# Routing stage of a linear-attention and mixture-of-experts layer: reordered input loads, layer-norm statistics by half blocks, one 1/sqrt per block, weight loads interleaved with the token stores

## The chip, the core and the metric

One core of one Trainium2 chip runs the whole program. The metric is the device time of one execution in microseconds (us). The kernel before was run three times: 717.43, 720.52 and 724.11 us, median 720.52 us.

The core has a matrix engine (TensorE, PE in the profile; its weight loads are shown as PEld), a vector engine (VectorE, DVE), an activation engine (ScalarE, ACT), a general engine (GpSimd, POOL) and SyncE (SP), which here only issues DMAs. Each engine executes its own instructions strictly in the order in which the program emitted them. DMAs issued by SyncE go on one hardware queue (q1 in the profile), those issued by ScalarE on another (q10).

## The reference

The input x has 4 x 1024 tokens of 256 channels. What matters here:

```python
xn = layernorm(x)                       # over 256 channels
# attention branch on xn: q, k, v projections, causal linear attention in
# chunks, a memory branch with gates, output projection w_o
# expert branch on xn:
logits = xn @ gate_weight.T             # 8 experts
scores = softmax(logits); topk_w, topk_idx = top_k(scores, 2)
topk_w = topk_w / (sum(topk_w) + 1e-20)
y  = sum over the two experts of topk_w * swiglu(xn, w_gate, w_up, w_down)
y += swiglu(xn, sw_gate, sw_up, sw_down)          # shared expert, all tokens
out = x + attention(xn) + y
```

The layer norm is (x - mean) / sqrt(var + 1e-5) for each token.

## The kernel before, in words

All arithmetic is fp32. The 4096 tokens are cut into 8 blocks (NBLK) of 512 (TB), each of 4 tiles (NT) of 128 tokens. The order of instructions on every engine is the order of the program text; no planner moves them. The kernel has four stretches:

1. **Loads** (lines 104 to 144). SyncE issues the eight blocks of x (512 KB each, L104), then the memories, gate, biases and most weights (L115 to L144). ScalarE issues `wvg` (value and expert-gate weights), `wq` and `wk`. On SyncE every store that follows comes behind all of these.
2. **The routing stage**, written out by hand as a list of steps, `ahead` (L1197). `S` is `statistics` of a block: four times bn_stats (L303) and bn_aggr (L304) on VectorE, an addition of epsilon (L309), and the power -1/2 on GpSimd (L312). Before the change, the addition and the power are done for two blocks at a time (blocks 1+2, 3+4, 5+6; 0 and 7 alone). `N` is `normalize`: a small `shift` (L319), two tiles normalized in place on VectorE (L326) and two on ScalarE (L331), and then one DMA that stores the block's normalized tokens to the DRAM tensor `xns` (L335), from which the experts later gather their rows. `T` is `transpose_x`: eight TensorE transposes by way of PSUM (L344), copied by ScalarE to `xnT` (L347). `V` is `values`: for each pair of tiles eight matmuls with `wvg` (L362), whose result ScalarE copies (L367, L371); GpSimd fills in ones and zeros (L372, L373). `masks`, `memories`, `gates`, `living` and `route` are small computations put between. The result of `pv` has two PSUM buffers (`ps_v`), each for one pair of tiles.
3. **Queries, keys, shared expert and sorting** (L1233 to L1237), in which TensorE projects queries and keys (L600) into four rotating PSUM banks (`ps_r`), ScalarE and VectorE turn them into elu(x)+1 (L605, L606, L614, L618), and VectorE sorts tokens into expert slots (`route(1)`, `sort`, `weights`, `owners`). In front of it SyncE issues the copies of x into the DRAM tensor `sums` and two fills from the SBUF tile `zero`:

```python
    for blk in range(NBLK):
        rows = slice(blk * TB, (blk + 1) * TB)
        nc.sync.dma_start(sums[rows, :], x[rows, :])
    nc.sync.dma_start(sums[T:, :], zero[:, :H])
    nc.sync.dma_start(xns[T:, :], zero[:, :H])
```

4. **Attention rounds with the routed experts beside them** (L1240 on), the bulk of the time.

Two sharings of buffers matter. The values of a block are written over its normalized tokens: `va` is a view of the tile `wide` that holds `xb`, so L367, L372 and L373 of a block have to wait until its `xns` store has read the block. And `zero` is one of three rotating buffers with the tag `wide` in the pool `tmp`, which the temporaries `eq` and `ek` of L605 use afterwards, so one of these has to wait until the last DMA that reads `zero` has finished.

Of the kernel before, what the change touches and what calls it, by code (L numbers as in the profile page):

```python
# [22 lines left out]
def linear_attention_moe_kernel(  # L23
# [28 lines left out]
    nc = tc.nc  # L52
    T, H = x.shape
    S = T // B
    NH = memory_gate.shape[1]
# [7 lines left out]
    FR = E * F  # L63
    FT = w_gate.shape[1]
    FS = FT - FR
# [3 lines left out]
    HID = eg_w1.shape[1]  # L69
    NBLK = T // TB  # L70
# [5 lines left out]
    NMN = 1 + NM  # L76
# [4 lines left out]
    const = ctx.enter_context(tc.tile_pool(name="const", bufs=1))  # L81
# [3 lines left out]
    small = ctx.enter_context(tc.tile_pool(name="small", bufs=2))  # L85
# [14 lines left out]
    def load_x(blk):  # L100

        wide = big.tile([P, NT, VW], FP, tag="tok", name=f"x_{blk}")
        xb = wide[:, :, :H]
        nc.sync.dma_start(  # L104
            xb, x[blk * TB : (blk + 1) * TB, :].rearrange("(n p) h -> p n h", p=P)
        )
        st["x", blk] = xb
        st["wide", blk] = wide

    for blk in range(NBLK):  # L110
        load_x(blk)

    def load_weight(w, name, engine=nc.sync):
        t = const.tile([P, NC, w.shape[1]], FP, tag=name, name=name)
        engine.dma_start(t, w.rearrange("(k p) c -> p k c", p=P))  # L115
        return t

    wvg = load_weight(w_vg, "wvg", nc.scalar)
    wq = load_weight(w_q, "wq", nc.scalar)
    wk = load_weight(w_k, "wk", nc.scalar)  # L120
    raw = const.tile([P, NC, NMN, D1], FP, tag="raw", name="raw")
    nc.sync.dma_start(
        raw[:, :, 1:NMN, :], memories.rearrange("(c p) m k -> p c m k", p=P)
    )
    gate = const.tile([P, NH], FP, tag="gate", name="gate")
    nc.sync.dma_start(gate, memory_gate.to_broadcast([P, NH]))
    b2 = const.tile([P, 1], FP, tag="b2", name="b2")
    nc.sync.dma_start(b2, eg_b2.to_broadcast([P, 1]))
    w1 = load_weight(eg_w1, "w1")
    b1 = const.tile([P, HID], FP, tag="b1", name="b1")  # L130
    nc.sync.dma_start(b1, eg_b1.rearrange("h o -> o h").to_broadcast([P, HID]))
    w2 = const.tile([P, HID], FP, tag="w2", name="w2")
    nc.sync.dma_start(w2, eg_w2.rearrange("h o -> o h").to_broadcast([P, HID]))
    wo = load_weight(w_o, "wo")
    wg = load_weight(w_gate[:, FR:], "wg")
    wu = load_weight(w_up[:, FR:], "wu")
    wd = const.tile([P, NF, H], FP, tag="wd", name="wd")
    full = FS // P
    nc.sync.dma_start(
        wd[:, :full, :],  # L140
        w_down[FR : FR + full * P, :].rearrange("(f p) h -> p f h", p=P),
    )
    if full < NF:
        nc.sync.dma_start(wd[: FS - full * P, full, :], w_down[FR + full * P :, :])  # L144


    zero = tmp.tile([P, TB], FP, tag="wide", name="zero", bufs=3)
# [6 lines left out]
    make_identity(nc, ident)  # L154
    ones = const.tile([P, P], FP, tag="ones", name="ones")
    nc.gpsimd.memset(ones, 1.0)
    neghalf = const.tile([P, 2 * NT], FP, tag="neghalf", name="neghalf")
    nc.gpsimd.memset(neghalf, -0.5)

    first = const.tile([P, E], FP, tag="first", name="first")  # L160
# [66 lines left out]
    ungate = const.tile([P, NH], FP, tag="ungate", name="ungate")  # L227
    gates = const.tile([P, H], FP, tag="gates", name="gates")

    def sigmoid(v):  # L230

        nc.scalar.activation(v, v, AF.Exp, scale=-1.0)
        nc.vector.tensor_scalar(v, v, 1.0, None, ALU.add)
        nc.vector.reciprocal(v, v)

    def masks():

        for r in range(2):
# [3 lines left out]
        for c in range(NC):  # L242
            nc.vector.tensor_copy(own_s[:, c], own[:, :, None].to_broadcast([P, HC, D1]))

    def gates_of_heads():
        nc.vector.tensor_scalar(gate, gate, -80.0, None, ALU.max)
        sigmoid(gate)
        nc.vector.tensor_scalar(ungate, gate, -1.0, 1.0, ALU.mult, ALU.add)
        nc.vector.tensor_copy(
            gates.rearrange("p (h k) -> p h k", k=HD), gate[:, :, None].to_broadcast([P, NH, HD])  # L250
        )
        nc.vector.tensor_scalar(b2, b2, 0.5, None, ALU.mult)
# [37 lines left out]
        nc.vector.tensor_scalar(alive, tot[:, :NMN], EPS, None, ALU.is_ge)  # L290


    def statistics(blk):

        xb = st["x", blk]
        if blk == 0 or blk % 2:
            st["mv"] = small.tile([P, 2, NT, 2], FP, tag="mv", name=f"mv_{blk}", bufs=3)
            st["rstd"] = small.tile([P, 2, NT], FP, tag="rstd", name=f"rstd_{blk}", bufs=3)
        mv, rstd = st["mv"], st["rstd"]
        at = (blk + 1) % 2 if blk else 0  # L300
        for i in range(NT):
            stats = small.tile([P, 6], FP, tag="stats", name=f"stats_{blk}_{i}")
            nc.vector.bn_stats(stats, xb[:, i, :])  # L303
            nc.vector.bn_aggr(mv[:, at, i, :], stats)  # L304
        st["norm", blk] = mv[:, at], rstd[:, at]
        if blk % 2 == 0 or blk == NBLK - 1:
            n = at + 1
            some = rstd[:, :n].rearrange("p b i -> p (b i)")
            nc.vector.tensor_scalar(  # L309
                some, mv[:, :n, :, 1].rearrange("p b i -> p (b i)"), LN_EPS, None, ALU.add  # L310
            )
            nc.gpsimd.tensor_tensor(some, some, neghalf[:, : n * NT], ALU.pow)  # L312

    def normalize(blk):

        xb = st["x", blk]
        mv, rstd = st.pop(("norm", blk))
        shift = small.tile([P, NT], FP, tag="shift", name=f"shift_{blk}")
        nc.vector.scalar_tensor_tensor(  # L319
            shift, mv[:, :, 0], -1.0, rstd, ALU.mult, ALU.mult  # L320
        )
        xnT = io.tile([P, NC, TB], FP, tag="xnT", name=f"xnT_{blk}")
        st["xnT", blk] = xnT
        half = NT // 2
        for i in range(half, NT):
            nc.vector.tensor_scalar(  # L326
                xb[:, i, :], xb[:, i, :], mv[:, i, 0:1], rstd[:, i : i + 1],
                ALU.subtract, ALU.mult,
            )
        for i in range(half):  # L330
            nc.scalar.activation(  # L331
                xb[:, i, :], xb[:, i, :], AF.Identity,
                bias=shift[:, i : i + 1], scale=rstd[:, i : i + 1],
            )
        nc.sync.dma_start(  # L335
            xns[blk * TB : (blk + 1) * TB, :].rearrange("(n p) h -> p n h", p=P), xb
        )

    def transpose_x(blk, pair):
        xb, xnT = st["x", blk], st["xnT", blk]  # L340
# [34 lines left out]
    def route(half):  # L375

        n = NTT // 2
        part = slice(half * n, (half + 1) * n)
        lg = lgs[:, part, :]
        sh = [P, n, E]  # L380

        def t2(name):
            return small.tile([P, n], FP, tag=name, name=f"{name}_{half}", bufs=2)

        def spread(t):
            return t[:, :, None].to_broadcast(sh)
# [12 lines left out]
        nc.vector.tensor_reduce(best, lg, AX.X, ALU.max)  # L399
        m1, m2 = (pick[r][:, part, :] for r in range(2))  # L400
        yield from first_largest(lg, best, m1, "m1")
        rest = small.tile(sh, FP, tag="rest", name=f"rest_{half}", bufs=1)
        nc.vector.scalar_tensor_tensor(rest, m1, -1e30, lg, ALU.mult, ALU.add)
        low = t2("low")
        nc.vector.tensor_reduce(low, rest, AX.X, ALU.max)
        yield from first_largest(rest, low, m2, "m2")
        st["best", half] = best
# [773 lines left out]
    def split(units, parts):  # L1181
# [12 lines left out]
        return runs  # L1194


    ahead = "S0 S1 masks N0 T0 S2 S3 N1 N2 V0 T1 T2 S4 memories V1 S5 N3 N4 V2 T3 T4 S6 gates V3 S7"  # L1197
    ahead += " N5 N6 V4 living T5 T6 N7 V5 route V6 T7 V7"
    other = {
        "masks": masks, "memories": memories_by_group, "gates": gates_of_heads, "living": living,  # L1200
        "route": lambda: [None for _ in route(0)],
    }
    with tc.tile_pool(name="ps_v", bufs=2, space=bass.MemoryType.PSUM) as ps_v:
        for what in ahead.split():
            if what in other:
                other[what]()
                continue
            blk = int(what[1:])
            if what[0] == "S":
                statistics(blk)  # L1210
            elif what[0] == "N":
                normalize(blk)
            else:
                for pair in range(NT // 2):
                    (transpose_x if what[0] == "T" else values)(blk, pair)

    ps_q = ctx.enter_context(tc.tile_pool(name="ps_q", bufs=1, space=bass.MemoryType.PSUM))
    quad = ps_q.tile([P, NG, 512], FP, tag="quad", name="quad")
# [128 lines left out]
```

## Time and profile before

| | |
|---|---|
| median of three runs | 720.52 us (717.43 to 724.11) |
| the profiled execution | 720.73 us, of which the span from first to last instruction is 718.8 us |
| mean granted TensorE clock | 0.97 |
| PE busy | 656.1 us, 91% of the span |
| PEld, DVE, ACT, POOL busy | 468.4, 455.8, 266.9, 385.6 us |
| DMA bytes over the span | 81.50 MB |
| first transposes start (L344) | 11.24 us |
| last value matmuls end (L362) | about 59.2 us |

The profile is one execution. The timeline lists instructions by start time (us from the span's start), then duration, engine, source line, operation and tiles (written<-read), and in brackets how long the engine had been idle and what ended the idle time. Neighbouring equal instructions are merged ("x8"), so a merged row's duration runs from the first start to the last end. "SPq" and "ACTq" are instructions that issue DMAs. Rows by window give each engine's busy time in a stretch, then the granted TensorE clock as a share of full speed and the DMA throughput.

### The profile page before, as it was taken

How to read it: one execution, taken by the hardware profiler on the slowest of the kernel's cores; microseconds unless marked ns; L12 is line 12 of the kernel's file. 1: busy time of each engine (PE TensorE's matmuls, PEld its weight loads, DVE VectorE, ACT ScalarE, POOL GpSimd, SP SyncE). 2: the span in 40 equal slices, each digit the busy share in tenths (PEclk: the TensorE clock that was granted, in tenths of full speed). 3: DMA queues.
4: the chain of work that ended last, by engine and by line, in shares of the span. 5: the costliest groups of instructions: out<-in, count | busy, mean ns of one | idle time of the engine just before them, and what ended most of it. 6: DMA issues, size and time to landing. Idle time of an engine off the chain costs nothing.

```text
span 718.8 us, 14242 instructions
## 1 busy us (share of the span) xinstructions
PE 656.1 (91%) x5084; PEld 468.4 (65%) x5084; DVE 455.8 (63%) x1193; ACT 266.9 (37%) x614; POOL 385.6 (54%) x436
## 2 busy tenths in 40 slices
PE   3699987888999999999999999999999987998987
PEld 2585465675676667766676766676767765665666
DVE  6544888886675656665756665657656654454764
ACT  3365443333433343334333442344333433243310
POOL 3210034455465566565664564646665777666576
PEclk9899988999999999999999999999999999699999
DMA  9556000014344444443444453535445676575285
GB/s 295 175 189 190 1 1 1 1 29 115 86 108 102 111 98 89 103 119 86 115 108 91 108 107 77 123 91 116 111 96 123 136 182 145 123 157 126 30 269 206
DMA packets 86466, 81.50 MB, mean 113 GB/s; under 512 B 7533, under 2 KB 83997, under 8 KB 86269
## 3 DMA queue, kind: packets, MB, share of 16 engines
q1 hardware_dynamic: 70797, 60.14, 29.1%
q0 software_dynamic: 13632, 18.62, 15.2%
q10 hardware_dynamic: 1968, 1.84, 0.7%
q8 instruction: 40, 0.66, 0.4%
q14 instruction: 29, 0.24, 0.1%
HBM read 62.62 MB, written 22.15 MB: 118 GB/s over the span
## 4 chain that ended last, share of the span: by engine, by line
PE 71%; DMA 9%; DVE 8%; POOL 4%; ACT 4%; issue 3%; SPq 0%; ACTq 0%; POOLq 0%; DVEq 0%
PE phe L1052 11%; PE pye L1065 7%; PE psu L921 6%; PE po L958 6%; PE pg L907 5%; DMA sums<-y,islot 4%; PE quad L691 4%; PE pn L717 4%; PE po L962 4%; PE quad L806 3%; PE pk L600 3%; PE pq L600 3%; PE pv L362 2%; PE pte L1039 2%; PE pte L1043 2%
## 5 line engine op out<-in xcount | busy, mean ns | idle before, releaser
L1074 POOL DMA_INDIRECT sums<-y,islot x71 | 113.3, 1595 | 80.0 <-DMA sums<-y,islot 28.4
L1052 PE MATMUL phe<-wgu,turned 128*128 128x352 f32 x276 | 99.5, 484 | 2.5 <-ACT turned L1045 1.2
L1058 DVE SCALAR_TENSOR_TENSOR hidden<-hidden,phe 128x176 f32<-128x176 f32 x71 | 23.8, 335 | 117.8 <-ACT hidden L1057 113.2
L698 DVE TENSOR_TENSOR sT<-quad,causal 128x512 f32<-128x512 f32 x128 | 80.6, 681 | 8.1 <-PE quad L691 7.8
L1006 POOL DMA_INDIRECT xg<-xns,islot x71 | 70.3, 990 | 19.7 <-issue 10.6
L1065 PE MATMUL pye<-wdn,turned 88*128 88x256 f32 x284 | 77.3, 395 | 1.8 <-issue 1.4
L828 POOL TENSOR_TENSOR cg<-coarse,gates 128x256 f32<-128x256 f32 x32 | 24.5, 767 | 98.0 <-DVE h L885 53.5
L1052 PEld LDWEIGHTS phe<-wgu,turned 128*128 128x128 f32 x276 | 49.5, 195 | 27.0 <-issue 8.3
L1065 PEld LDWEIGHTS pye<-wdn,turned 88*128 88x128 f32 x284 | 51.2, 194 | 15.3 <-issue 6.7
L1069 ACT ACTIVATE y<-pye,wslot 128x256 f32<-128x256 f32 x71 | 33.6, 473 | 70.8 <-PE pye L1065 59.0
L1045 ACT COPY turned<-pte 128x512 f32<-128x512 f32 (+1 forms) x71 | 41.0, 578 | 46.7 <-PE pte L1043 43.1
L846 POOL TENSOR_TENSOR fm<-fm 128x512 f32<-128x512 f32 x32 | 44.0, 1374 | 26.7 <-DVE prob L894 16.6
L1057 ACT ACTIVATE hidden<-phe 128x176 f32<-128x176 f32 x71 | 22.5, 317 | 71.3 <-PE phe L1052 67.6
L958 PE MATMUL po<-wd,h 128*128 128x256 f32 (+1 forms) x192 | 47.4, 383 | 0.1
L907 PE MATMUL pg<-xnT,wg 128*128 128x512 f32 (+1 forms) x96 | 47.4, 617 | 0.0
L921 PE MATMUL psu<-xnT,wu 128*128 128x512 f32 (+1 forms) x96 | 47.0, 613 | 0.2 <-DVE skT L618 0.2
L835 DVE TENSOR_TENSOR fm<-quad,rw 128x512 f32<-128x512 f32 x64 | 41.9, 680 | 0.0
L560 POOL TENSOR_TENSOR held<-ones,two 128x213 f32<-128x213 f32 (+1 forms) x22 | 16.0, 736 | 44.9 <-DVE ones L540 44.9
L896 DVE SCALAR_TENSOR_TENSOR o<-diff,prob,loc 128x256 f32<-128x256 f32 x32 | 37.4, 1167 | 3.4
L362 PE MATMUL pv<-wvg,xnT 128*128 128x264 f32 x128 | 32.9, 418 | 7.0 <-ACT xnT L347 7.0
L958 PEld LDWEIGHTS po<-wd,h 128*128 128x128 f32 (+1 forms) x192 | 34.9, 190 | 6.4 <-issue 0.4
L806 PE MATMUL quad<-mem,sqT 32*128 32x170 f32 x512 | 28.9, 341 | 7.6 <-DVE sT L698 7.5
(210 smaller groups left out, 1376.1 us busy)
## 6 DMA issues: line engine op xcount, KB each, us to landing
wgu<-in_w_gate_dram SPq DMA_DIRECT2D x71, 176.0 KB
wgu<-in_w_up_dram SPq DMA_DIRECT2D x71, 176.0 KB
wdn<-in_w_down_dram SPq DMA_DIRECT2D x71, 176.0 KB
x<-in_x_dram SPq DMA_DIRECT2D x8, 512.0 KB
xns<-x SPq DMA_DIRECT2D x8, 512.0 KB
sums<-in_x_dram SPq DMA_DIRECT2D x8, 512.0 KB
part<-sums SPq DMA_DIRECT2D x12, 256.0 KB
out_dram<-acc SPq DMA_DIRECT2D x12, 256.0 KB
```

The source lines that it names most:

```text
L362: nc.tensor.matmul(pv[:, j, : H + E], xnT[:, k, i * P : (i + 1) * P], wvg[:, k, :], start=(k == 0), stop=(k == NC - 1),)
L600: nc.tensor.matmul(pq, w[:, k, c * P : (c + 1) * P], xnT[:, k, :], start=(k == 0), stop=(k == NC - 1),)
L698: nc.vector.tensor_mul(sT, quad[:, g, :].rearrange("p (c t) -> p c t", t=P), causal[:, None, :].to_broadcast([P, NC * 2, P]),)
L806: nc.tensor.matmul(quad[:, g, c * KM : (c + 1) * KM], sqT[rows, c, tok], mem[rows, c, :], start=True, stop=True,)
L846: nc.gpsimd.tensor_add(fm[:, :, 0:2, :], fm[:, :, 0:2, :], fm[:, :, 2:4, :])
L907: nc.tensor.matmul(pg[:n, :], wg[:, k, f * P : f * P + n], xnT[:, k, :], start=(k == 0), stop=(k == NC - 1),)
L921: nc.tensor.matmul(pu[:n, :], wu[:, k, f * P : f * P + n], xnT[:, k, :], start=(k == 0), stop=(k == NC - 1),)
L958: nc.tensor.matmul(po[:, :H], st["h", blk, f][:k, tok], wd[:k, f, :], start=(f == 0), stop=False)
L1006: nc.gpsimd.indirect_dma_start(out=xg, out_offset=None, in_=xns, in_offset=bass.IndirectOffsetOnAxis(ap=islot[:, j : j + 1], axis=0),)
L1052: nc.tensor.matmul(ph[:, : 2 * F], xgT[:, k, :], wgu[:, k].rearrange("p g f -> p (g f)"), start=(k == 0), stop=(k == NC - 1),)
L1065: nc.tensor.matmul(py[:, :H], hT[:FH, f, :], wdn[:, f, :], start=(f == 0), stop=(f == 1))
L1074: nc.gpsimd.indirect_dma_start(out=sums, out_offset=bass.IndirectOffsetOnAxis(ap=islot[:, j : j + 1], axis=0), in_=st.pop(("y", j)), in_of ...
```

## The change

- Block 0 of x is loaded as two halves, the first on SyncE's queue, the second on ScalarE's. `wvg` follows on ScalarE's queue.
- All other constants are no longer issued behind x. They are collected in a list, `loads`, in a new order, and `normalize` issues two of them after every `xns` store. So on SyncE the stores come right behind the x loads.
- `statistics` works on half a block (two tiles) at a time; epsilon and the power are done once for every block, after its second half.
- The list `ahead` is new: the halves stand about the normalizations, values go pair by pair with the next block's transposes between them, and `masks`, `memories`, `living`, `route` and `gates` are put elsewhere.
- The exponential of the head gates becomes a step of its own (`exps`), apart from what VectorE does with it (`gates`).

```diff
+        parts = 2 if blk == 0 else 1
+        n = NT // parts
+        for part in range(parts):
+            rows = slice((blk * NT + part * n) * P, (blk * NT + (part + 1) * n) * P)
+            (nc.scalar if part else nc.sync).dma_start(
+                xb[:, part * n : (part + 1) * n],
+                x[rows, :].rearrange("(n p) h -> p n h", p=P),
+            )
...
+    def load_weight(w, name, engine=None):
+        t = const.tile([P, NC, w.shape[1]], FP, tag=name, name=name)
+        src = w.rearrange("(k p) c -> p k c", p=P)
+        if engine is None:
+            loads.append(lambda: nc.sync.dma_start(t, src))
+        else:
+            engine.dma_start(t, src)
+        return t
+
+    load_x(0)
+    wvg = load_weight(w_vg, "wvg", nc.scalar)
+    for blk in range(1, NBLK):
         load_x(blk)
...
-    def statistics(blk):
+    def statistics(blk, half):
...
+        n = NT // 2
+        for i in range(half * n, (half + 1) * n):
             stats = small.tile([P, 6], FP, tag="stats", name=f"stats_{blk}_{i}")
             nc.vector.bn_stats(stats, xb[:, i, :])
-            nc.vector.bn_aggr(mv[:, at, i, :], stats)
...
+            nc.vector.bn_aggr(mv[:, i, :], stats)
+        if half:
+            nc.vector.tensor_scalar(rstd, mv[:, :, 1], LN_EPS, None, ALU.add)
+            nc.gpsimd.tensor_tensor(rstd, rstd, neghalf, ALU.pow)
...
         nc.sync.dma_start(
             xns[blk * TB : (blk + 1) * TB, :].rearrange("(n p) h -> p n h", p=P), xb
         )
+        for _ in range(2):
+            if loads:
+                loads.pop(0)()
...
-    ahead = "S0 S1 masks N0 T0 S2 S3 N1 N2 V0 T1 T2 S4 memories V1 S5 N3 N4 V2 T3 T4 S6 gates V3 S7"
-    ahead += " N5 N6 V4 living T5 T6 N7 V5 route V6 T7 V7"
+    ahead = "S0a S0b S1a N0 T0 S1b S2a N1 V0a T1 V0b S2b S3a N2 V1a T2 V1b masks S3b S4a N3 V2a T3 V2b"
+    ahead += " memories S4b S5a N4 V3a T4 V3b living S5b S6a N5 V4a T5 V4b route exps S6b S7a N6 V5a T6"
+    ahead += " V5b S7b N7 V6a T7 V6b gates V7a V7b"
```

The order of `loads` is: memories (`raw`), gate; wq, wk; b2, wg; wu, w1; b1, w2; wo, the first part of wd; the rest of wd. So the store of block 0 has the first two behind it, that of block 1 the next two, and so on; block 7's has none.

More of the change, by code (lines that the diff above doesn't have):

```diff
@@ L103, in load_x @@
         xb = wide[:, :, :H]
-        nc.sync.dma_start(
-            xb, x[blk * TB : (blk + 1) * TB, :].rearrange("(n p) h -> p n h", p=P)
-        )
+        parts = 2 if blk == 0 else 1
[6 more added lines that the diff above has]
+            )
@@ L107, in load_x @@
         st["x", blk] = xb
         st["wide", blk] = wide
-    for blk in range(NBLK):
-        load_x(blk)
[L113 to L120, printed above, removed]
+    loads = []
+    def load_weight(w, name, engine=None):
[6 more added lines that the diff above has]
+        return t
@@ L121, in linear_attention_moe_kernel @@
+    load_x(0)
+    wvg = load_weight(w_vg, "wvg", nc.scalar)
+    for blk in range(1, NBLK):
+        load_x(blk)
     raw = const.tile([P, NC, NMN, D1], FP, tag="raw", name="raw")
-    nc.sync.dma_start(
-        raw[:, :, 1:NMN, :], memories.rearrange("(c p) m k -> p c m k", p=P)
+    loads.append(
+        lambda: nc.sync.dma_start(
+            raw[:, :, 1:NMN, :], memories.rearrange("(c p) m k -> p c m k", p=P)
+        )
     )
     gate = const.tile([P, NH], FP, tag="gate", name="gate")
-    nc.sync.dma_start(gate, memory_gate.to_broadcast([P, NH]))
+    loads.append(lambda: nc.sync.dma_start(gate, memory_gate.to_broadcast([P, NH])))
@@ L127, in linear_attention_moe_kernel @@
+    wq = load_weight(w_q, "wq")
+    wk = load_weight(w_k, "wk")
     b2 = const.tile([P, 1], FP, tag="b2", name="b2")
-    nc.sync.dma_start(b2, eg_b2.to_broadcast([P, 1]))
+    loads.append(lambda: nc.sync.dma_start(b2, eg_b2.to_broadcast([P, 1])))
+    wg = load_weight(w_gate[:, FR:], "wg")
+    wu = load_weight(w_up[:, FR:], "wu")
     w1 = load_weight(eg_w1, "w1")
     b1 = const.tile([P, HID], FP, tag="b1", name="b1")
-    nc.sync.dma_start(b1, eg_b1.rearrange("h o -> o h").to_broadcast([P, HID]))
+    loads.append(
+        lambda: nc.sync.dma_start(b1, eg_b1.rearrange("h o -> o h").to_broadcast([P, HID]))
+    )
@@ L132, in linear_attention_moe_kernel @@
     w2 = const.tile([P, HID], FP, tag="w2", name="w2")
-    nc.sync.dma_start(w2, eg_w2.rearrange("h o -> o h").to_broadcast([P, HID]))
+    loads.append(
+        lambda: nc.sync.dma_start(w2, eg_w2.rearrange("h o -> o h").to_broadcast([P, HID]))
+    )
     wo = load_weight(w_o, "wo")
-    wg = load_weight(w_gate[:, FR:], "wg")
-    wu = load_weight(w_up[:, FR:], "wu")
     wd = const.tile([P, NF, H], FP, tag="wd", name="wd")
     full = FS // P
-    nc.sync.dma_start(
-        wd[:, :full, :],
-        w_down[FR : FR + full * P, :].rearrange("(f p) h -> p f h", p=P),
+    loads.append(
+        lambda: nc.sync.dma_start(
+            wd[:, :full, :],
+            w_down[FR : FR + full * P, :].rearrange("(f p) h -> p f h", p=P),
+        )
@@ L142, in linear_attention_moe_kernel @@
     )
     if full < NF:
-        nc.sync.dma_start(wd[: FS - full * P, full, :], w_down[FR + full * P :, :])
+        loads.append(
+            lambda: nc.sync.dma_start(
+                wd[: FS - full * P, full, :], w_down[FR + full * P :, :]
+            )
+        )
     zero = tmp.tile([P, TB], FP, tag="wide", name="zero", bufs=3)
@@ L156, in linear_attention_moe_kernel @@
     nc.gpsimd.memset(ones, 1.0)
-    neghalf = const.tile([P, 2 * NT], FP, tag="neghalf", name="neghalf")
+    neghalf = const.tile([P, NT], FP, tag="neghalf", name="neghalf")
     nc.gpsimd.memset(neghalf, -0.5)
@@ L228, in linear_attention_moe_kernel @@
     gates = const.tile([P, H], FP, tag="gates", name="gates")
[L230 to L234, printed above, removed]
     def masks():
@@ L243, in masks, with exp_gates @@
             nc.vector.tensor_copy(own_s[:, c], own[:, :, None].to_broadcast([P, HC, D1]))
+    def exp_gates():
+        nc.vector.tensor_scalar(gate, gate, -80.0, None, ALU.max)
+        nc.scalar.activation(gate, gate, AF.Exp, scale=-1.0)
     def gates_of_heads():
-        nc.vector.tensor_scalar(gate, gate, -80.0, None, ALU.max)
-        sigmoid(gate)
+        nc.vector.tensor_scalar(gate, gate, 1.0, None, ALU.add)
+        nc.vector.reciprocal(gate, gate)
         nc.vector.tensor_scalar(ungate, gate, -1.0, 1.0, ALU.mult, ALU.add)
@@ L290, in living @@
         nc.vector.tensor_scalar(alive, tot[:, :NMN], EPS, None, ALU.is_ge)
-    def statistics(blk):
+    def statistics(blk, half):
         xb = st["x", blk]
[L296 to L301, printed above, removed]
+        if half == 0:
+            st["norm", blk] = (
+                small.tile([P, NT, 2], FP, tag="mv", name=f"mv_{blk}", bufs=3),
+                small.tile([P, NT], FP, tag="rstd", name=f"rstd_{blk}", bufs=3),
+            )
+        mv, rstd = st["norm", blk]
+        n = NT // 2
+        for i in range(half * n, (half + 1) * n):
             stats = small.tile([P, 6], FP, tag="stats", name=f"stats_{blk}_{i}")
             nc.vector.bn_stats(stats, xb[:, i, :])
-            nc.vector.bn_aggr(mv[:, at, i, :], stats)
[L305 to L312, printed above, removed]
+            nc.vector.bn_aggr(mv[:, i, :], stats)
+        if half:
+            nc.vector.tensor_scalar(rstd, mv[:, :, 1], LN_EPS, None, ALU.add)
+            nc.gpsimd.tensor_tensor(rstd, rstd, neghalf, ALU.pow)
     def normalize(blk):
@@ L1194, in split @@
         return runs
-    ahead = "S0 S1 masks N0 T0 S2 S3 N1 N2 V0 T1 T2 S4 memories V1 S5 N3 N4 V2 T3 T4 S6 gates V3 S7"
-    ahead += " N5 N6 V4 living T5 T6 N7 V5 route V6 T7 V7"
+    ahead = "S0a S0b S1a N0 T0 S1b S2a N1 V0a T1 V0b S2b S3a N2 V1a T2 V1b masks S3b S4a N3 V2a T3 V2b"
+    ahead += " memories S4b S5a N4 V3a T4 V3b living S5b S6a N5 V4a T5 V4b route exps S6b S7a N6 V5a T6"
+    ahead += " V5b S7b N7 V6a T7 V6b gates V7a V7b"
     other = {
-        "masks": masks, "memories": memories_by_group, "gates": gates_of_heads, "living": living,
-        "route": lambda: [None for _ in route(0)],
+        "masks": masks, "memories": memories_by_group, "exps": exp_gates, "gates": gates_of_heads,
+        "living": living, "route": lambda: [None for _ in route(0)],
     }
@@ L1207, in linear_attention_moe_kernel @@
                 continue
-            blk = int(what[1:])
+            blk, half = int(what[1]), "ab".find(what[2:])
             if what[0] == "S":
-                statistics(blk)
+                statistics(blk, half)
             elif what[0] == "N":
                 normalize(blk)
-            else:
-                for pair in range(NT // 2):
-                    (transpose_x if what[0] == "T" else values)(blk, pair)
+            elif what[0] == "T":
+                for pair in range(NT // 2):
+                    transpose_x(blk, pair)
+            else:
+                values(blk, half)
+    assert not loads
     ps_q = ctx.enter_context(tc.tile_pool(name="ps_q", bufs=1, space=bass.MemoryType.PSUM))
```

## The prediction

> **What bounds the kernel now.** The page's first part has TensorE busy for 656.1 of 718.8 us, so a change of the first 60 us can count only by when the later stages start. I read the timeline of the first 100 us, then the same stretch by windows, then the chain of waits in order of time.
>
> The timeline shows why the routing stage is slow (bracket: idle before, releaser):
>
> ```profile
> 11.24 2.04 PE L344 MATMUL pt<-ident,x 128*128 128x128 f32 x8 [11.24 <-ACT x L331]
> ...
> 19.09 30.03 SPq L335 DMA_DIRECT2D xns<-x  x8
> ...
> 25.26 0.59 ACT L367 COPY x<-pv 128x512 f32<-128x512 f32 x1 [7.43 <-DMA xns<-x]
> ...
> 27.03 8.95 PE L362 MATMUL pv<-wvg,xnT 128*128 128x264 f32 x32 [6.66 <-ACT xnT L347]
> ```
>
> The store of block 0 is issued at 19.09, since SyncE issues all constants first; it lands at 25.2; ScalarE's copy of the first values waits for it (7.43 us), the copies to xnT stand behind that copy, and TensorE idles 6.66 us.
>
> The windows (busy time by engine, granted clock, DMA share, GB/s) give the load rate and what idling does to the clock:
>
> ```profile
> 0.00:5.00 5.00, 0.00 (x0) 0.00 (x0) 0.00 (x0) 0.00 (x0) 4.02 (x31) 1.00 0.58 184
> 5.00:10.00 5.00, 0.00 (x0) 0.00 (x0) 4.15 (x17) 1.28 (x1) 1.05 (x1) 1.00 1.09 369
> 10.00:15.00 5.00, 3.76 (x12) 2.95 (x13) 4.73 (x23) 2.26 (x4) 1.38 (x1) 1.00 1.09 366
> 15.00:20.00 5.00, 5.00 (x28) 4.33 (x27) 4.71 (x21) 2.08 (x4) 0.27 (x1) 1.00 0.81 211
> 20.00:25.00 5.00, 0.37 (x4) 0.12 (x2) 3.55 (x23) 0.00 (x0) 0.00 (x0) 0.84 1.06 370
> 25.00:30.00 5.00, 2.97 (x7) 2.36 (x8) 2.71 (x11) 3.19 (x8) 2.44 (x13) 0.50 0.35 124
> ```
>
> But the chain of waits does not leave the stage by TensorE. It goes from the last token store into the copies to `sums` and the last fill from `zero`:
>
> ```profile
> 48.77 0.36 SPq L335
> 49.18 0.64 SPq L1221
> 49.87 6.01 DMA sums<-in_x_dram
> 55.90 10.72 DMA xns<-zero
> 66.72 0.60 ACT eq L605
> ```
>
> and the timeline there:
>
> ```profile
> 66.72 0.60 ACT L605 ACTIVATE eq<-pq 128x512 f32<-128x512 f32 x1 [2.82 <-DMA xns<-zero]
> ...
> 68.77 0.32 PEld L600 LDWEIGHTS pk<-xnT,wk 128*128 128x128 f32 x2 [0.54 <-DVE sqT L614]
> ```
>
> The third `eq` needs the buffer of `zero`, and so waits 2.82 us for the last DMA; TensorE is hurt by only 0.54 us, because it still had filled PSUM banks to work through. So at 66.7 us two paths are nearly level: TensorE's, and the DMAs', which start with the store of block 7 (48.77) and end 17.9 us later.
>
> **Part by part.**
>
> *Loads and stores.* Ahead of block 0's store stood 6.54 MB of loads; after the change it is x and wvg, 4.19 + 0.27 = 4.46 MB. By the windows 0.92 + 1.845 + 1.83 = 4.6 MB have moved by 15.0, so these end at 14.6; the store (0.524 MB at 0.37 MB/us) ends at 16.0. Before, the same sum gives 23.8 for the store, and it landed at 25.2, so I add 1.35: 17.4 instead of 25.2. Its issue (SyncE is through with x at 9.9 before) is early enough. The later stores have at most 0.52 MB of weights between them, and 1.05 MB take 2.8 us of a block's 4.5. One that was issued at 44.23 beside another landed at 48.1, 3.9 us; alone it is 3.9 less half to all of the other's 1.4, some 3 us. It must land before its block's first value copy, one block (4.45 us) later: hidden, with a cover of a little over 1 us. The constants are needed later than they land: memories at about 23 (land about 18), wq after 53 (about 20).
>
> *Two halves of block 0.* First statistics start at 5.54 when block 0 has landed. Halves save between 0 (the other half shares the DMA engines) and about 1.4 us (0.262 of 0.524 MB, with as much of ScalarE's queue beside it). I take 1.1. The Trainium skill ("DMA: Bandwidth & Descriptors", Rules for kernel authors) says not to bother with halves on two queues, since all queues run on the same 16 DMA engines and interleave; by it this is worth nothing. Either value is hidden, because TensorE next waits for 17.4.
>
> *Statistics and order.* Before the first transposes, VectorE had 16 bn instructions and masks between arrival and shift (5.54 to 10.40). Now 12 (3.2 us) and the power beside them: transposes at about 8.9 instead of 11.2. Then values of block 0, transposes and second half, until about 17; the store lands at 17.4, ScalarE copies values (0.54) and the first half of xnT (0.6), and the values of block 1 start at 18.5 instead of 27.0. The three extra powers (1.05 us each for a block against 1.65 for two) run beside the next half's statistics (1.06), save 0.2 to 0.3 us of latency each that I count below.
>
> From there TensorE needs 1.78 a half block of values (7.12/4) and 0.9 a block of transposes: 4.45 a block. VectorE needs 2.2 + 0.7 = 2.9 a block, so it keeps up where nothing else stands in its queue. Two things do. *living* now stands in front of S5b; its comparison waits for a TensorE product behind V3b:
>
> ```profile
> 45.22 0.17 DVE L290 TENSOR_SCALAR alive<-tot 128x5 f32<-128x5 f32 x1 [1.74 <-PE tot L287]
> ```
>
> Before, only one shift and what follows stood behind it. Now, with V3b ending at 31.9 (18.5 + 5 x 1.78 + 3 x 0.9 + 1.8 for V3b) and the product at 32.3, S5b, the power and N5 follow: 32.5 + 1.1 + 0.3 + 1.1 = 35.1 for the shift, and T5, due at 34.1, starts at 35.9, 2 us lost with ScalarE's second tile. Then *route* (3.5 us, 46.06 to 49.6 in the timeline) stands between N5 and S6b: 35.8 + 3.5 + 0.15 + 1.05 + 0.35 + 1.05 + 0.1 = 42.0 for the shift of N6; T6, due at 40.6, starts at 42.7, again 2 us. N7's second ScalarE tile follows V5b's copy, at 47.3. The stage ends at 53.7 instead of 59.2: **5.5 us gained on TensorE, but only 1.4 us at the last store** (47.4 against 48.77).
>
> *What comes next.* The copies start 1.4 us earlier and take their 17.9, so the `eq` goes at 65.3, and TensorE's next key product at 67.4 instead of 68.8. TensorE, 5.5 earlier (68.77 + 0.1 for the end of the product before it, less 5.5), has used its banks by 63.4: it now idles some 3.8 us. So 1.4 is what is kept, and the idle time has a price, the clock. By windows of 3.41 us (the spacing of the clock's changes in this trace):
>
> ```profile
> 125.79:129.21 3.42, 1.86 (x38) 1.73 (x38) 3.32 (x9) 0.96 (x4) 2.70 (x4) 1.00 0.00 0
> 129.21:132.62 3.41, 3.41 (x17) 1.97 (x12) 3.41 (x6) 1.31 (x4) 2.64 (x4) 0.50 0.00 0
> ```
>
> A window with 1.86 of 3.42 us busy was followed by one at half clock. 3.8 us of idle time leave one such window wherever the boundaries fall, and then 2.7 to 6 us of work run at half clock: 1.4 to 3 us lost, less about 1 us which the chain (VectorE until 72.6, TensorE only from there) lets pass: 0.4 to 2, I take 1.2. The Trainium skill ("TensorE: Matmul & The Clock Gate", Part 1) has the clock fall after an idle window of about 3.4 us; if only a wholly idle window counted, a gap of 3.8 us would mostly cost nothing, and the sum would be 1.2 us less. The row with 54% busy decides for me. The same can befall T6 and V5b after their 2 us pause, 0 to 1.7 us at N7; I take 0.7. Before the change the 6.66 us pause cost 1.66 (8.95 against 7.29 for 32 products); that lies in the 5.5.
>
> Gates, exps and the moved masks: under 1 us of VectorE each where it waits anyway; nothing, or 0.3 if the cover is gone.
>
> Sum against the profiled 720.73: -1.4 + 1.2 + 0.7 = +0.5, 721.2; the median of the runs lies 0.2 lower: **721.0**.
>
> **Rivals.** *The 5.5 us arrive whole*: if the `eq` does not wait for the fills, or N7 comes 4 us sooner because VectorE is not held by living and route, 720.7 - 5.5 = 715.2 (712 to 717 with the clock). For: TensorE's own path really gets that much. Against: the 2.82 us row, and DMA traffic that ends at the same moment.
> *Slower, by the stores*: each block's value copies wait for a store, on ScalarE in front of the next transposes' copies. The price is 1 us a block for each us that a store takes over 4.45 us from its block's normalization, for seven blocks, and the `sums` copies begin as much later: at 5.5 us 7.3 us, 728. It decides from 4.45 us. For: ScalarE and GpSimd waited for these stores at 25.3, 28.0 and 48.2, and two loads now lie between any two of them. Against: the bytes, 2.8 us of 4.45.
> *It does nothing*: TensorE and DMAs as level as before, 720.5; that is within my forecast.
>
> **How the numbers follow.** Forecast (715 to 726, the two clock terms at both ends, the store at 17.4 plus or minus 1.5, runs that spread by 3 us to either side) 0.62; whole gain 0.23; stores 0.15. Within 1% (7.2 us; smaller is no sure difference here) lie nearly all of the first, somewhat over half of the second and a third of the third. Faster by over 1%: 0.02 + 0.11 = 0.13; slower: 0.02 + 0.10 = 0.12; the rest 0.75. The range 714 to 727 leaves out about 0.1 at each end.
>
> **What would show it.** Right: block 0's store lands near 17.4; first transposes near 9; pauses of TensorE of about 2 us before T5 and T6, with alive released by tot and then route on VectorE; last `xns` store issued at 47 to 49; an `eq` released by xns<-zero after 6 us rather than 2.82, and half a clock behind it. Wrong: N7's store before 45, or no wait of `eq` for the fill, or value copies that wait for stores in every block.

## The result, and the profile after

No difference that can be measured: the changed kernel has a median of 723.0 us (714.46 to 726.04, 20 runs), the kernel before in the same series 722.98 us (717.43 to 726.43, 20 runs); ratio 0.9997, 95% interval 0.9976 to 1.0019, that is, -1.7 to +1.4 us. The profiled execution of the changed kernel has a span of 722.7 us and is one of the longer ones; the one of before, 718.8 us, is one of the shorter. Their difference of 4 us lies within what executions of one kernel differ by.

Inside this equal time the first 70 us are quite different. The timeline of the changed kernel (columns as before; lines of the new file: L366 transposes, L384 value matmuls, L389 value copies, L622 and L627 query and key products and `eq`):

```profile
9.11 2.03 PE L366 MATMUL pt<-ident,x 128*128 128x128 f32 x8 [9.11 <-ACT x L350]
...
17.57 0.59 ACT L389 COPY x<-pv 128x512 f32<-128x512 f32 x1 [4.79 <-DMA xns<-x]
...
18.77 2.05 PE L384 MATMUL pv<-wvg,xnT 128*128 128x264 f32 x8 [1.89 <-ACT xnT L369]
...
32.73 0.17 DVE L312 TENSOR_SCALAR alive<-tot 128x5 f32<-128x5 f32 x1 [3.86 <-PE tot L309]
...
36.21 1.47 PE L366 MATMUL pt<-ident,x 128*128 128x128 f32 x8 [1.64 <-ACT x L350]
...
67.03 0.60 ACT L627 ACTIVATE eq<-pq 128x512 f32<-128x512 f32 x1 [8.15 <-DMA xns<-zero]
...
69.07 3.78 PE L622 MATMUL pk<-xnT,wk 128*128 128x512 f32 x4 [5.09 <-DVE sqT L636]
```

The reader should compare row by row with before. First transposes 9.1 instead of 11.2. Block 0's store has landed at 17.6 instead of 25.3, and the values of block 1 start at 18.8 instead of 27.0, 8.3 us sooner. Then VectorE waits 3.86 us in `living`, and TensorE 1.64 us for the transposes of block 5 (T5). The last rows are the point: `eq`, which waited 2.82 us for the fill from `zero`, now waits 8.15 us for it, and goes at the same time as ever, 67.0 against 66.7. TensorE, which had lost 0.54 us there, now idles 5.09.

The chain of waits of the changed kernel, at the same place:

```profile
47.87 0.37 SPq L354
...
48.97 6.33 DMA sums<-in_x_dram
55.31 11.64 DMA xns<-zero
...
67.03 0.61 ACT eq L627
```

The last token store is issued 0.9 us earlier than before (47.87 against 48.77), although the last value matmul starts 5.0 us earlier (53.8 against 58.8). From the store to `eq` it is 19.2 us; before it was 17.9. And the windows show what the idle time does to the clock:

```profile
54.00:70.00 16.00, 10.79 (x26) 4.78 (x25) 6.31 (x20) 5.99 (x12) 0.00 (x0) 0.94 0.62 187
68.00:75.00 7.00, 5.93 (x7) 2.52 (x8) 6.29 (x20) 3.74 (x7) 0.00 (x0) 0.51 0.00 1
```

TensorE is busy for 10.8 of 16 us in front, and then works at a granted clock of 0.51, 7 matmuls in 7 us; in the kernel before it was 1.00 from 68 to 75 us, with 17 matmuls. The first `found` product (the lists for the experts) comes at 96.8, 2.7 us later than before.

### The profile page after: what moved, and what is told of

Same layout as the page of the kernel before. It is cut to its first block, busy times and chain, and to the rows that moved or that the text cites. A ratio compares the mean times of both kernels' runs of the same rounds, so it can differ in the third digit from the quotient of the medians.

```text
span 722.7 us, 14253 instructions
## 1 busy us (share of the span) xinstructions
PE 659.9 (91%) x5084; PEld 469.4 (65%) x5084; DVE 454.3 (63%) x1196; ACT 268.0 (37%) x614; POOL 387.5 (54%) x439
## 4 chain that ended last, share of the span: by engine, by line
PE 70%; DMA 10%; DVE 6%; POOL 6%; ACT 3%; issue 3%; SPq 0%; POOLq 0%; ACTq 0%; DVEq 0%
PE phe L1074 11%; PE pye L1087 7%; PE pg L929 6%; PE po L980 6%; PE psu L943 5%; DMA sums<-y,islot 5%; PE pk L622 4%; PE quad L713 4%; PE po L984 4%; PE pn L739 3%; PE quad L828 3%; PE pq L622 3%; PE pv L384 2%; PE ph L903 2%; PE pte L1061 2%
## 5 line engine op out<-in xcount | busy, mean ns | idle before, releaser
L1028 POOL DMA_INDIRECT xg<-xns,islot x71 | 70.7, 995 | 21.3 <-issue 8.8
L1074 PEld LDWEIGHTS phe<-wgu,turned 128*128 128x128 f32 x276 | 49.2, 194 | 27.1 <-issue 7.6
L929 PE MATMUL pg<-xnT,wg 128*128 128x512 f32 (+1 forms) x96 | 49.4, 639 | 0.0
L1079 ACT ACTIVATE hidden<-phe 128x176 f32<-128x176 f32 x71 | 22.6, 318 | 70.6 <-PE phe L1074 70.4
L918 DVE SCALAR_TENSOR_TENSOR o<-diff,prob,loc 128x256 f32<-128x256 f32 x32 | 35.9, 1123 | 3.4
L622 PE MATMUL pk<-xnT,wk 128*128 128x512 f32 x64 | 33.1, 644 | 5.1 <-DVE sqT L636 5.1
L1065 PE MATMUL pte<-ident,xg 128*128 128x128 f32 x138 | 27.2, 280 | 9.9 <-DMA xg<-xns,islot 9.9
```

Source lines behind the costliest of these rows:

```text
L622: nc.tensor.matmul(pq, w[:, k, c * P : (c + 1) * P], xnT[:, k, :], start=(k == 0), stop=(k == NC - 1),)
L929: nc.tensor.matmul(pg[:n, :], wg[:, k, f * P : f * P + n], xnT[:, k, :], start=(k == 0), stop=(k == NC - 1),)
L1028: nc.gpsimd.indirect_dma_start(out=xg, out_offset=None, in_=xns, in_offset=bass.IndirectOffsetOnAxis(ap=islot[:, j : j + 1], axis=0),)
L1074: nc.tensor.matmul(ph[:, : 2 * F], xgT[:, k, :], wgu[:, k].rearrange("p g f -> p (g f)"), start=(k == 0), stop=(k == NC - 1),)
```

## The experiments

Theory: the stage gained 5 us on TensorE, which the fill from `zero` takes back, because that fill is queued behind the last token store, and VectorE holds this store up with `living` and `route`; the half clock behind the wait costs 1 to 3 us more. Rivals: the gain is used up by the sorting and the lists later, or the change's two parts gain nothing in themselves. In all runs a ratio is to the kernel before, run beside it on the same chip, with its 95% interval. It need not equal the quotient of two medians (for e7 0.9878, where the medians give 0.990), and the kernel before had a median of 723.63 us beside e1 to e4, 724.19 beside e5 to e8 and 721.47 beside e9 to e12, so medians of different groups are not to be compared. "Last values" is the start of the last value matmul, "first found" that of the first `found` product. The times in the last four columns are from each run's profile, us from the span's start ("never": it does not wait for the fill).

| run | median us | ratio | last values | last store | eq after the fill | first found |
|---|---|---|---|---|---|---|
| before | 722.98 | | 58.8 | 48.8 | 66.7 | 94.1 |
| after | 723.0 | 0.9997 (0.9976 to 1.0019) | 53.8 | 47.9 | 67.0 | 96.8 |
| e1 after, own zero | 715.74 | 0.9896 (0.9862 to 0.9931) | 53.7 | 47.8 | never | 88.6 |
| e2 before, own zero | 723.1 | 0.9988 (0.9959 to 1.0016) | 58.5 | 48.5 | never | 93.4 |
| e3 after, living and route later | 715.65 | 0.9891 (0.9851 to 0.9931) | 49.6 | 43.3 | 62.5 | 91.7 |
| e4 after, 12 products more | 729.36 | 1.0066 (1.0034 to 1.0098) | 53.7 | 47.8 | 66.6 | 98.8 |
| e5 after, 6 products more | 725.17 | 1.0015 (0.9991 to 1.0038) | 55.5 | 49.6 | 68.5 | 95.9 |
| e6 both, e1 and e3 | 715.15 | 0.9863 (0.9837 to 0.989) | 50.8 | 44.5 | never | 85.7 |
| e7 own zero, loads alone | 717.0 | 0.9878 (0.9843 to 0.9912) | 49.2 | 39.2 | never | 84.1 |
| e8 own zero, list alone | 728.96 | 1.0076 (1.0046 to 1.0107) | 62.7 | 56.8 | never | 97.6 |
| e9 after again | 721.85 | 1.0002 (0.9981 to 1.0022) | 54.0 | 48.1 | 65.8 | 94.4 |
| e10 as e5, beside e9 | 722.59 | 1.0001 (0.9985 to 1.0017) | 55.4 | 49.5 | 68.2 | 95.6 |
| e11 e1, block 0 whole | 713.29 | one run | 53.6 | 47.7 | never | 88.4 |
| e12 e6, store 0 on ScalarE's queue | 712.18 | 0.986 (0.984 to 0.988) | 49.0 | 42.6 | never | 83.8 |

**The wait for the fill (e1, e2).** In both kernels one line:

```diff
-    zero = tmp.tile([P, TB], FP, tag="wide", name="zero", bufs=3)
+    zero = const.tile([P, H], FP, tag="zero", name="zero")
```

> The changed kernel with the zero tile in a buffer of its own, so that no temporary of the projections has to wait for the fills. Theory (the fill from the zero tile bounds the next stage): the third eq goes at about 59 instead of 67.0, TensorE's second key product at about 63.8 instead of 69.1, and no half clock follows; 5 to 7 us less than the kernel before, 716 to 718 where that has 723. Rival (a later stage, sorting or the lists on VectorE and GpSimd, has the same bound anyway): the wait goes, and the total stays within 2 us.

> The kernel before with the zero tile in a buffer of its own. Theory (both paths were level at 66.7 us): eq no longer waits 2.8 us, VectorE's sorting steps behind it move up by up to 3 us, TensorE by 0.5; 0 to 1.5 us less, 721.5 to 723. Rival (the copies alone bounded the kernel before): 3 us less, 720.

With it the changed kernel is 7.5 us faster than the kernel before (ratio 0.9896); the kernel before gains nothing that can be told (0.9988, interval over 1). In e1's profile the stretch behind the routing stage reads

```profile
62.07 3.60 PE L622 MATMUL pk<-xnT,wk 128*128 128x512 f32 x8
```

```profile
54.00:70.00 16.00, 15.90 (x40) 7.29 (x39) 11.94 (x37) 8.62 (x15) 0.00 (x0) 1.00 0.61 184
```

The first row is from its timeline: both key products in one run of eight rows, where the changed kernel had four and then a pause. The second is from its windows: 15.9 of 16 us busy at full clock, against 10.8 at 0.94. So the wait for the fill is what takes the change's gain, and it is no loss in the kernel before, where TensorE arrives no sooner. The rival, that a later stage has the same bound anyway, falls with 7.5 us.

**What the last store waits for (e3).** `living` and `route` moved behind the last normalization:

```diff
-    ahead += " memories S4b S5a N4 V3a T4 V3b living S5b S6a N5 V4a T5 V4b route exps S6b S7a N6 V5a T6"
-    ahead += " V5b S7b N7 V6a T7 V6b gates V7a V7b"
+    ahead += " memories S4b S5a N4 V3a T4 V3b S5b S6a N5 V4a T5 V4b exps S6b S7a N6 V5a T6"
+    ahead += " V5b S7b N7 living route V6a T7 V6b gates V7a V7b"
```

> The changed kernel with living and route moved behind N7; the zero tile is shared as in the changed kernel. Theory (on VectorE living's wait for TensorE and route hold up N5 and N6, and with them the last token store, from which the copies and the fill are reckoned): no pauses of TensorE before T5 and T6, last store at about 42.7 instead of 47.9, the third eq at about 62 instead of 67.0; 4 to 5 us less than the changed kernel, 718 to 719. Rival (the copies take until about 67 whenever they start, for instance because the token stores in front of them are late): eq stays at 67, total 722 to 723.

From its timeline:

```profile
43.30 0.37 SPq L354 DMA_DIRECT2D xns<-x  x1
...
62.47 0.60 ACT L627 ACTIVATE eq<-pq 128x512 f32<-128x512 f32 x1 [7.71 <-DMA xns<-zero]
```

The last store comes 4.6 us earlier and `eq` with it, 62.5; the wait stays nearly as long, 7.71 us, since TensorE's values end earlier as well (49.6). The total falls by 1.1%, about 8 us, where 4 to 5 were expected. That the copies always end at about 67 is refuted: the fill follows the store by 19 us. Within the intervals the earlier end of the copies is worth as much as the removed wait. But this profile shows only part of it: its first `found` product is 2.4 us before that of the kernel before (91.7 against 94.1), and it is that of the slowest of the six executions, 722.78 us where the median is 715.65. Where the rest of the 8 us comes from is not shown.

**The half clock (e4, e5, e9, e10).** Products that nothing reads, into a PSUM bank not yet in use, fill TensorE's pause:

```diff
+    def keep_warm():
+        for _ in range(12):
+            nc.tensor.matmul(
+                quad[:, 0], wk[:, 0, :P], st["xnT", 0][:, 0, :], start=True, stop=True
+            )
```

put in front of the second key product; e5 and e10 have `range(6)`.

> The changed kernel with 12 additional products of 512 columns in front of the second key product, whose result nothing reads; they fill TensorE's idle time of 5 us. Theory (part of the loss is the half clock after the idle time, 68.1 to 74.9): eq still goes at 67.0, the clock stays at 1.0 there, 1 to 2.5 us less than the changed kernel, 720.5 to 722. Rival (the clock costs nothing, because VectorE bounds this stretch): no difference, 723.

> As the run kept warm, with 6 additional products instead of 12 in front of the second key product (in that run a product of 512 columns took 0.86 us in two passes, so 12 filled 10.5 us instead of 5). Theory (the half clock behind the idle time costs TensorE's chain 2.5 to 3 us: from the second key product to the first found product it was 27.8 us in the changed kernel, 24.8 in the run kept warm): the second key product stays at about 69, no half clock at 68, the first found product at about 94 instead of 96.8; total 2 to 3 us under the changed kernel, about 720. Rival (VectorE's sorting bounds this stretch, and the run kept warm was only shifted): found stays near 96.8, total 723.

> The changed kernel unchanged, beside the kernel before and the next run on one chip. Theory: a ratio within 0.3% of 1, eq at about 67, half clock behind it; the stretch from the second key product to the first found product 26 to 28 us, by where the clock's windows fall.

> The kernel with 6 additional products once more, now beside the changed kernel on the same chip. If the half clock behind the wait costs the whole program what it costs the stretch (25.2 us there against 27.8), it is 1.5 to 3 us faster than the changed kernel. Rival (the gain is used up later, or the products themselves cost something): the same or slower; in the first run it was 725.2 where the changed kernel had 723.0 on another chip.

e4 was mis-sized, as its profile shows:

```profile
63.73 10.46 PE L1265 MATMUL quad<-xnT,wk 128*128 128x512 f32 x24
```

Each of the 12 products has two rows and takes 0.86 us, so they ran 5 us past the pause; the run is slower than the kernel before by 0.66%, 4.8 us. It still tells that without half clock it is 24.8 us from the second key product (74.0) to the first `found`, where the changed kernel needs 27.8 (69.1 to 96.8). With six products (e10's windows) TensorE is busy throughout and the clock stays:

```profile
62.00:72.00 10.00, 10.00 (x26) 4.47 (x25) 2.29 (x8) 3.46 (x6) 0.00 (x0) 1.00 0.30 103
```

and the stretch takes 25.2 us in e5 (70.7 to 95.9) and 25.0 in e10 (70.6 to 95.6); in e9, the changed kernel once more, 26.6 (67.9 to 94.4). In the kernel before, at full clock, it was 25.3, from the weight load at 68.8 to 94.1. So against e5 and e10 the half clock costs this stretch 1.4 to 2.8 us. The rows of e9 at the wait:

```profile
65.81 0.60 ACT L627 ACTIVATE eq<-pq 128x512 f32<-128x512 f32 x1 [6.70 <-DMA xns<-zero]
...
67.86 2.81 PE L622 MATMUL pk<-xnT,wk 128*128 128x512 f32 x4 [3.65 <-DVE sqT L636]
```

But neither e5 nor e10 is faster: side by side on one chip 722.59 with the products and 721.85 without, both level with before. The expectation fails for the total. In both profiles with six products the clock had fallen to half once before, in the pause in front of block 1's values (2.46 and 2.29 us, where e9 has 1.59), which put the last store at 49.5; the two profiles of the changed kernel do not have that. The products, issued some 45 us later, are not needed for it: e6 below has none and shows the same fall after a pause of 2.56 us. Whether it is the reason for the equal totals, these runs do not settle, so what the half clock costs in the total stays open.

**The parts of the change (e7, e8).** Both have the zero tile in its own buffer, so that the fill hides nothing, and are to be read against e2 (neither part) and e1 (both). e7 has of the change only the halves of block 0, the stores behind x, and the weight loads behind the stores; statistics, powers for two blocks and the old list stay. e8 has only the statistics by halves, the power for every block, `exps` and the new list.

> The kernel before with the zero tile in its own buffer and of the change only the new order of loads and stores (halves of block 0, weight loads behind the stores); statistics and list of steps as before. Theory (the first store's landing sets the stage): block 0's store lands at 17 to 18, second block's values start at about 19.5 instead of 27, no half clock there; last values at 51 to 54; total 6 to 8 us under the kernel before. Rival (the old list needs its power for two blocks and its wait for the gates, so the stage is held by VectorE): last values at 57 or later, total within 3 us of the kernel before.

> The kernel before with the zero tile in its own buffer and of the change only the statistics by halves, the power for every block and the new list of steps; loads as before. Theory: block 0's store is issued at about 19 and lands at 25, values of block 1 start at about 26.5; with the pauses at living and route the last values end at 61 to 62; total 1 to 4 us over the kernel before. Rival (the list alone is worth the gain): last values at 56 or earlier, total 5 us under.

The first row is from e7's timeline (its L388 are the value matmuls), the next from e8's (L358):

```profile
18.99 7.39 PE L388 MATMUL pv<-wvg,xnT 128*128 128x264 f32 x32 [0.28 <-ACT xnT L373]
```

```profile
25.73 3.88 PE L358 MATMUL pv<-wvg,xnT 128*128 128x264 f32 x8 [7.10 <-ACT xnT L343]
```

With the loads alone block 1's values start at 19.0 after a pause of 0.28, at full clock, the old list goes on without holding up its normalizations, and the last store is issued at 39.2: 1.2% faster than before. With the list alone TensorE waits 7.1 us for the same late store, then loses more at `living` and `route`, and the last store comes at 56.8: 0.8% slower, 5.5 us (3.3 to 7.7), where 1 to 4 were expected. So, within these intervals, all of the gain is in the order of loads and stores, and nothing is to be seen of the new list: both parts together (e1, ratio 0.9896) are level with the loads alone (0.9878), though their first `found` product comes 4.5 us later (88.6 against 84.1). The loads alone with the shared `zero` tile were not run.

**Halves of block 0 (e11).** `parts = 1` in e1.

> The changed kernel with the zero tile in its own buffer and block 0 loaded whole on SyncE's queue. Theory: first statistics at 5.1 to 5.6 instead of 4.6, first transposes up to 1 us later than 9.1; block 1's values still start at about 18.8, because they wait for block 0's store; total as with the halves, 715 to 718.

```profile
5.49 0.43 DVE L327 BATCH_NORM_STATS2 stats<-x 128x6 f32<-128x256 f32 x1 [5.49 <-DMA x<-in_x_dram]
```

The halves bring the first statistics forward by 0.9 us (4.58 in the changed kernel) and the first transposes by 0.8 (9.1 against 9.9). Block 1's values start at 18.6, no later than with halves. The total of 713.29 us is that of a single run; it says nothing against this and proves nothing.

**A version that beats both (e6, e12).** e6 is e1 and e3 together; e12 sends block 0's token store by ScalarE's queue in addition:

```diff
-        nc.sync.dma_start(
+        (nc.scalar if blk == 0 else nc.sync).dma_start(
             xns[blk * TB : (blk + 1) * TB, :].rearrange("(n p) h -> p n h", p=P), xb
```

> The changed kernel with the zero tile in a buffer of its own and living and route behind N7. Theory: last values at about 49, no wait for the fill and no half clock there, the first found product at about 84 instead of 96.8; 10 to 12 us less than the kernel before, 711 to 713. Rival (the two gains are one and the same, each of them had about 7.5): 715 to 716.

> The kernel with the zero tile in its own buffer and living and route behind N7, and in addition block 0's token store on ScalarE's queue, so that it does not stand behind the rest of x. Theory (engines take the queues in turns): the store lands at 13 to 14.5 instead of 17.5, block 1's values start at about 17 instead of 18.8, TensorE has no pause there, so no half clock; the first found product 1 to 3 us earlier than 85.7; total 0 to 3 us under the run with both. Rival (the store's bytes still queue behind x): no difference.

e6 takes 715.15 us. By its ratio it is 1.4% under before, 9.9 us (8.0 to 11.8), where the theory had 10 to 12; but the median is the one that the rival forecast (715 to 716, the two gains being one and the same). Its interval overlaps those of e1 and e3, and the loads alone (e7, 0.9878) are level with it. So it is not shown that the gains add up. Its `found` comes 8.4 us before that of the kernel before; in its profile block 1's values ran at half clock (3.74 us for a half block instead of 2.05), 1.7 us lost there. e12 has the same ratio, 0.986. Its store was hardly sooner:

```profile
9.66 0.38 ACTq L354 DMA_DIRECT2D xns<-x  x1
...
17.19 0.59 ACT L389 COPY x<-pv 128x512 f32<-128x512 f32 x1 [4.33 <-DMA xns<-x]
```

Issued at 9.7 on the other queue, it landed at 17.2, as against 17.6 behind x. The transfers by queue of e12 (packets, MB, share of 16 engines), between 9.6 and 13.7 us, and then between 13.7 and 17, show why:

```profile
q1 hardware_dynamic: 1438, 1.43, 108.9%
```

```profile
q1 hardware_dynamic: 994, 0.69, 65.1%
q10 hardware_dynamic: 528, 0.52, 45.4%
```

For 4 us after the issue only SyncE's queue moves bytes; then the two share. Up to 13.7 us SyncE's queue had moved 3.43 of its 3.93 MB of x. So most of what it had issued before went first, but not all: the last half megabyte of x shares with the store. What ended the 4 us is not shown.

## Why the prediction was right

*That TensorE's gain is not kept, since the way out of the stage is by the last store, the copies and the fill*: right, and shown by e1, e2 and e3. Its times came out close. (The forecast total of 721.0 us started from a median of 720.52; the longer series of the kernel before has 722.98, so the ratio is what to compare.)

| step | predicted | measured |
|---|---|---|
| first transposes | 8.9 | 9.1 |
| block 0's store landed | 17.4 | 17.6 |
| values of block 1 | 18.5 | 18.8 |
| last store issued | 47.4 | 47.9 (48.1 in e9) |
| eq released by the fill | 65.3 | 67.0 (65.8 in e9) |
| TensorE's second key product | 67.4 | 69.1 (67.9 in e9) |
| idle time there | 3.8 | 5.1 (3.65 in e9) |

*The order of VectorE's queue*: right. `alive` waits 3.86 us for TensorE with S5b behind it, T5 comes at 36.2 (35.9 predicted), and moving both steps brings the last store 4.6 us forward (e3). One detail was otherwise: in the profile after, the pause before T5 put TensorE at half clock (16 value matmuls in 5.35 us instead of 3.73), so that T6 came when TensorE had only just finished: a pause of 0.18 us there. In e9, at full clock, T5 had the same pause of 1.64 us and T6 one of 1.86, as predicted. Two sums of the prediction are slightly off, and nothing rests on them: the shift at 35.1 adds up to 35.0, and the idle time of 3.8 is 4.0 by its own 67.4 and 63.4.

*The copies take 17.9 us from the last store*: about 1 us too little. In the six profiles of the changed kernel and its variants with the shared `zero` tile (after, e3, e4, e5, e9, e10) it is 17.7 once, in e9, and 18.7 to 19.2 otherwise. So of the 1.4 us that the prediction let through, nothing was left at `eq` in the profile after (67.0 against 66.7), and 0.9 in e9.

*The clock, 1.2 us after the wait and 0.7 at T6 and V5b*: the fall of the clock after the wait came as stated. For the stretch it was meant for, the term is 1.4 to 2.8 us; in the total no run shows it. The 0.7 was nothing: in the profile after the clock did fall behind T5's pause, and the last store was issued at 47.87; in e9 it did not, and the store was issued at 48.09, since T6 starts at 43.0 and 43.2 all the same, held up by the normalization behind `route`.

Taken together, the first `found` product comes 2.7 us later than before in the profile after, and 0.3 us in e9; the prediction's terms add up to +0.5, and the total moved by 0.0, with an interval of -1.7 to +1.4. Even the -1.4 alone would lie in that interval. So the total confirms that nothing much is gained or lost, but not the sizes of the terms, and that they cancel so closely is partly luck.

*Halves of block 0*: 1.1 us predicted at the start and nothing in the end; 0.9 and nothing. The Trainium skill ("DMA: Bandwidth & Descriptors", Rules for kernel authors) says not to bother with two transfers of disjoint partition halves, and that spreading DMAs over queues doesn't help bandwidth. The halves here are halves of the tokens, over all partitions. That nothing came of them in the end agrees with it (block 1's values at 18.6 without halves, 18.8 with them); but the first half was there 0.9 us sooner. For the clock, the skill's table ("TensorE: Matmul & The Clock Gate", Part 1) has half clock after at least one idle window of about 3.4 us. Read as a window without any work, this is too mild here: in the trace of before, a window with 1.86 of 3.42 us busy was followed by half clock, and after T5's pause of 1.64 us in the profile after, 16 value matmuls took 5.35 us instead of 3.73.

*The rivals*: the whole gain of 5.5 us did not come, and e1 shows under which condition it does: the prediction named it, an `eq` that does not wait for the fills (7.5 us, interval 5.0 to 10.0). Stores that hold up the values in every block: no. In the changed kernel ScalarE waits for a store only at 17.6, and GpSimd after that for at most 1.3 us (at 46.7).

## What to carry to other kernels

When a stage is sped up, look for what at its end hangs on another event than the engine that was sped up: here a DMA that reads a rotating buffer, level with TensorE before the change and alone on the path after it. A buffer that a long DMA reads should not be in a pool whose next user is on the path; here one line turned a change that brought nothing into a gain of 7.5 us, while it did nothing that can be told for the kernel before. And in a hand-written order, a step that waits for another engine, or a long one, belongs behind the steps that others wait for (e3).

## What was not expected

A store issued on a second queue waited for most of what the first had already issued: none of its bytes moved for 4 us (9.7 to 13.7, 1.43 MB of x went first), after which the two queues shared.

The time from the first gather for the experts to the end of the span is not a constant: 551.6 us before, 554.0 after, 551.8 in e1, 557.1 in e3, 559.7 in e7, 550.3 in e9. After and e9 are one kernel, so some 4 us of this lies between executions, and one profile each does not rank the kernels. e7's first gather comes at 156.0, 11.2 us before that of the kernel before, and in the two profiles 3.1 us of it are left at the end; by the ratio e7 gains 8.8 us (6.4 to 11.4), so whether its usual execution loses any of the 11.2 is not shown. A stretch that is 1.6 us shorter, as in e10, need not show in a total at all. Which wait in the expert rounds makes the difference was not tried.
